# A graph layer on one core: sums stored by SyncE, a buffer for each gather, tables kept between turns, and sorted ranges of 8192 edges

## The chip, the cores and the metric

The kernel runs on one core of a Trainium2 chip. The core has five engines with instruction streams of their own: TensorE (PE; its weight loads are shown apart as PEld), VectorE (DVE), ScalarE (ACT), GpSimd (POOL) and SyncE (SP, which here issues DMAs alone). They share 16 DMA engines, an on-chip memory (SBUF, with PSUM for the products of TensorE) and the chip's HBM. The metric is the time of one execution on the device, in microseconds, as the median of several runs.

## The reference

The input is a table `x` of 100,000 nodes with 64 features, and 3,300,000 edges (`src`, `dst`), sorted by destination. The edges are 1,600,000 random pairs in both directions and one edge from each node to itself. The inputs are made from seed 0.

```
h   = relu(layernorm(x))
y_e = W @ [h[dst_e], h[src_e] - h[dst_e]] + b        for each edge e
s   = segment_sum(y, dst);  cnt = number of edges of each node
out = x + where(cnt > 0, s / max(cnt, 1), 0)
```

The product with `W` is linear, so it may be applied after the mean over a node's edges. What costs is the sum over edges of `h[src]` for each destination.

## The kernel before

Rows of `h` are kept in HBM as `h3`: three bf16 parts that add up to the float32 value, then a column of ones that counts edges. Sums go to an accumulator `acc` in HBM, 65 float32 values for each node.

The edges are divided in two. The first 256 x 7936, in the order of their destinations, make 256 *ranges* (`NW` = 256, one row of `src_w` and `dst_w` each). A range has `WL` = 8192 places; the last `PAD` = 256 hold a key `END` that sorts behind all edges. The rest of the edges, in the order of their destinations too, make 354 *chunks* of 28 x 128 edges (`NCH`, `J` = 28).

A range's sums go to `CH` = 256 rows of nodes from the range's first destination on. Chunks use 128 rows in the same way. Several tests write into a tile `odd` whether the data fit such a layout:

- lines 443 to 446: a range's last destination minus its first must be below `CH`;
- lines 628 and 629: a range may hold at most 256 edges from a node to itself;
- others hold for chunks (line 250), for counts of edges between a range and a block of sources, and for positions.

Lines 959 to 967 take the maximum over all tests as `turns`: a number of clearings, 0 or 1, and a number of passes of a general loop, 0 or `NF` = edges / 2048 rounded up.

The stages, in order of time:

1. *Opening* (lines 199 to 304): layer norm, `h3`, a float32 copy `hb`, and zeros into `acc`.
2. *Sort* (`sort_windows`): each range is sorted by source with a bitonic network on DVE and ACT, one range per half partition. Meanwhile POOL gathers rows for chunks.
3. *Pass 0* (`passes(0, ...)`, written out in full). For the 40 source blocks of group 0, tables (`tab`) of `h3` lie in SBUF. A set is four ranges, a pass does all 64 sets. Each block of a set takes `pick` (one-hot product on PE that picks the source rows), a copy by ACT to bf16, and `put` (one-hot product that adds rows into `total` in PSUM by destination). After 40 blocks `total` goes through `whole` and a reduction to `wsums`, and these partial sums go to `part_d` in HBM.
4. *Turns*: a loop of three for groups 1 to 3, then a loop of two *final halves* for group 4, with 32 sets each. A final set adds its sums to `acc`.
5. *General loop* (lines 1005 to 1055): if `turns` says so, `acc` is cleared, and then all edges are done again, 2048 in each of `NF` passes. A pass loads indices, gathers 16 x 128 rows, makes one-hot products, and adds the 16 results to `acc` with indirect accumulating DMAs issued by POOL. With data that fit, both loops run zero times.
6. *Closing stage* (lines 1057 to 1093): `acc`, `hb` and `x` are read, divided, multiplied by the weights and stored.

Chunks run beside all this as an event stream (`chunks`, line 347): one indirect gather on POOL (line 399), and, `LAGJ` = 21 gathers later, one product on PE (line 410). A pass interleaves them by a written-out rate: pass 0 by `STEP`, turns by the number of chunks `KB` = 64 that each owns. The gathers go to buffers `nb` of seven (`JN`), six such buffers in rotation. After 28 gathers the sums of a chunk (`sums`) are added to `acc` by POOL: an indirect accumulating DMA in the static part (line 368), an accumulating DMA to a loaded address in the loops (line 373). The sums of final sets go the same way (line 922). `add_later` and `add_now` hold these adds back until 14 gathers later, with at least `GAP` = 4 gathers between two of them. `in_turn`, `behind` and `issue_after` fix an instruction's place in its engine's order.

SP issues nearly all loads: `srs` and `dt` (sources and destinations of a block for the one-hots, fetched ten blocks ahead), `prev` (partial sums), `tab` at the start of each turn, the chunks' indices `si` and `di`, and the stores of `wsums` to `part_d`. At the edge of a loop all engines drain and meet.

Of the kernel before, what the change touches and what calls it, by code (L numbers as in the profile page):

```python
# [28 lines left out]
P = 128  # L29
# [3 lines left out]
KB = 64  # L33
KG = 8
JN = 7
JH = 14
LAG = 3
LAGJ = 21
GATHER = 1270
STEP = 900  # L40
GAP = 4
# [12 lines left out]
PAD = 256  # L54
# [39 lines left out]
def gnn_preln(ctx: ExitStack, tc, x, src_w, dst_w, src_p, dst_p, src_a, dst_a, wT, b, out, V, E):  # L94
# [35 lines left out]
    RT = max(R, NCB * CS)  # L130
# [6 lines left out]
    assert 2 * C == P and NX * P >= 2 * CH and PA >= 0 and KB % 2 == 0  # L137
# [6 lines left out]
    acc = dram.tile([R, C1], F32, name="acc")  # L144
# [3 lines left out]
    ksort = dram.tile([NW * WL, 1], I32, name="ksort")  # L148
# [34 lines left out]
    odd = consts.tile([P, 3 + 2 * NL + 2], F32, name="odd")  # L183
# [3 lines left out]
    hb_v = hb.rearrange("(p t) c -> p t c", p=P)  # L187
    h3_v = h3[:R].rearrange("(p t) c -> p t c", p=P)
    acc_v = acc.rearrange("(p t) c -> p t c", p=P)
# [9 lines left out]
    with tc.tile_pool(name="pre", bufs=2) as pre, tc.tile_pool(name="small", bufs=4) as small, \  # L199
# [11 lines left out]
        zeros = pre.tile([P, T, C1], F32, name="zeros", bufs=1)  # L211
        nc.gpsimd.memset(zeros, 0.0)
        for r in range(R, RT, P):
            n = min(P, RT - r)
            nc.scalar.dma_start(h3[r:r + n], zeros.rearrange("p t c -> p (t c)").bitcast(BF16)[:n, :CT])
# [90 lines left out]
    with tc.tile_pool(name="rows", bufs=6) as rows, \  # L306
# [40 lines left out]
        def chunks(first, n, dynamic=None):  # L347


            def load(q):  # L350
# [5 lines left out]
                nc.sync.dma_start(di[:, :k], dst_p[at].rearrange("k p j -> p k j"))  # L356
# [5 lines left out]
                to = index.tile([P, KG], I32, name="to", bufs=3)  # L362
                nc.vector.tensor_scalar(to[:, :k], base_b[:, at], pcol, None, op0=ALU.add)
                return si, near, to

            def addition(q, rows_to, sums):
                if dynamic is None:
                    nc.gpsimd.indirect_dma_start(
                        out=acc, out_offset=bass.IndirectOffsetOnAxis(ap=rows_to, axis=0),
                        in_=sums, in_offset=None, compute_op=ALU.add)  # L370
                else:
                    at = number(base_r[0:1, ds(dynamic + q, 1)], POOL, V)
                    nc.gpsimd.dma_start(acc[ds(at, P)], sums, accum_op=ALU.add)  # L373
# [15 lines left out]
            for e in range(n * J + LAGJ):  # L389
                q, j = divmod(e, J)  # L390
                u = q % KG
                if e < n * J:
                    if j == 0:
                        if u == 0:
                            si, near, to = ahead
                        of[q] = u, si, near, to
# [7 lines left out]
                if d + JN >= 0 and (d + JN) % JH == 0:  # L404
                    hot_of(d + JN)
# [724 lines left out]
```

## Time and profile before

| what | value |
|---|---|
| median of 3 runs | 16331.0 us (16321.65 to 16351.86) |
| the profiled execution | 16308.1 us |
| its span | 16306.4 us |
| instructions | 639004 |
| gathers of chunks (line 399) | 9912, 1025 ns mean, 10159.1 us in all |
| HBM read, written | 1655.06 MB, 255.11 MB |

The stages begin at about 0 (opening), 410 (sort), 2530 (slots are filled), 2707 (pass 0), 5261, 7782 and 10289 (turns), 12790 and 14403 (final halves) and 15993 us (closing stage).

In the groups of instructions, a row gives the line, the engine, the operation, what it writes and reads, the shapes and the count; then busy time and mean duration of one; then the idle time of the engine just before, and what ended most of it. "issue" is time in which nothing that the profile shows was waited for. A row of waits says who waited for whom, the total in us, the number of waits and the longest. A row of the timeline gives the start, the duration, the instruction, and in brackets the engine's idle time before it and what ended that. A row of a stretch gives busy time and count for PE, PEld, DVE, ACT and POOL, then the clock granted to TensorE, the DMA share and GB/s.

### The profile page before, as it was taken

The numbers are of one execution on the slowest core, as the hardware profiler recorded it, in microseconds if no ns is written. First come the engines' busy times: TensorE is split into PE (matmuls) and PEld (weight loads), VectorE is DVE, ScalarE is ACT, GpSimd is POOL, SyncE is SP. The second block draws the span as 40 slices with busy tenths as digits, with TensorE's granted clock in tenths as the row PEclk, the third lists the DMA queues.
The fourth block names the chain that finished last, engine by engine and source line by source line (L and its number), as shares of the span: only waits on it lengthen the run. The fifth ranks groups of instructions, "written<-read, shape, count | busy, mean of one in ns | idle before, by whom it ended". The sixth has DMA issues, their size and how long they took to land. (4 is left out here: it accounts for less than half of the span.)

```text
span 16306.4 us, 639004 instructions
## 1 busy us (share of the span) xinstructions
PE 12051.6 (74%) x266300; PEld 9566.6 (59%) x266300; DVE 12400.5 (76%) x31837; ACT 7270.1 (45%) x15555; POOL 11887.4 (73%) x11203
## 2 busy tenths in 40 slices
PE   6111113899996988898888899788899777767775
PEld 5001012777774777776777777677777666556654
DVE  6999997888884877787777788677788666656663
ACT  6234393555553444444444444444444333333331
POOL 4777777776656777777777777777777777767766
PEclk7555556999997999999999999899999888988887
DMA  7311124444444545554544455544455544455447
GB/s 294 82 39 39 40 59 107 121 124 124 126 123 106 126 125 125 125 127 113 144 122 125 124 127 126 130 122 125 125 128 127 128 106 106 106 117 108 106 104 260
DMA packets 1639658, 1952.46 MB, mean 120 GB/s; under 512 B 1039558, under 2 KB 1040206, under 8 KB 1631758
## 3 DMA queue, kind: packets, MB, share of 16 engines
q1 hardware_dynamic: 1178128, 1341.28, 27.4%
q0 software_dynamic: 454560, 544.34, 18.5%
q8 instruction: 2086, 34.18, 0.8%
q10 hardware_dynamic: 4032, 25.69, 0.4%
q14 instruction: 852, 6.98, 0.1%
HBM read 1655.06 MB, written 255.11 MB: 117 GB/s over the span
## 5 line engine op out<-in xcount | busy, mean ns | idle before, releaser
L399 POOL DMA_INDIRECT nb<-h,si x9912 | 10159.1, 1025 | 3436.5 <-issue 2642.3
L870 ACT CAST gs<-gp 128x386 bf16<-128x386 f32 x12800 | 5570.9, 485 | 7102.0 <-PE gp L865 6961.0
L342 DVE TENSOR_TENSOR dh<-dt,upto 128x512 bf16<-128x512 int16 x12800 | 4582.1, 420 | 1797.4 <-PE total L877 1660.3
L877 PE MATMUL total<-gs,dh 32*128 32x193 bf16 x200704 | 5465.0, 247 | 408.0 <-DVE whole L907 377.6
L865 PE MATMUL gp<-tab,gh 128*128 128x193 bf16 x50176 | 5419.6, 250 | 349.3 <-DVE gh L844 227.6
L865 PEld LDWEIGHTS <-gh 128*128 128x128 bf16 x51200 | 4487.9, 99 | 1410.2 <-issue 967.4
L877 PEld LDWEIGHTS <-dh 32*128 32x128 bf16 x200704 | 3997.4, 94 | 1479.3 <-issue 926.8
L410 PE MATMUL ps<-nb,hot 128*128 128x193 bf16 x9912 | 2231.0, 274 | 3012.8 <-DMA nb<-h,si 1519.6
L844 DVE TENSOR_SCALAR gh<-srs,who_f 128x768 bf16<-128x768 int16 (+1 forms) x10240 | 3414.6, 396 | 981.2 <-PE gp L865 846.8
L410 PEld LDWEIGHTS <-hot 128*128 128x128 bf16 x9912 | 862.6, 103 | 3281.0 <-issue 1654.0
L471 ACT COPY tmp<-keys 128x1536 f32<-128x1536 f32 (+26 forms) x525 | 647.7, 1244 | 1044.8 <-DVE keys L473 880.4
L342 DVE TENSOR_TENSOR hot<-near,upto 128x512 bf16<-128x512 int16 (+1 forms) x2832 | 915.8, 385 | 68.1 <-PE ps L410 67.5
L472 DVE TENSOR_TENSOR keys<-tmp,keys 128x1536 f32<-128x1536 f32 (+26 forms) x525 | 748.0, 1462 | 68.3 <-ACT tmp L471 67.2
L473 DVE TENSOR_TENSOR keys<-tmp,keys 128x1536 f32<-128x1536 f32 (+26 forms) x525 | 750.3, 1460 | 1.1
L910 DVE TENSOR_REDUCE wsums<-whole 128x512 f32<-128x1536 f32 x320 | 614.5, 1920 | 0.2
L765 POOL DMA_INDIRECT kw<-ksort,at x392 | 427.3, 1090 | 211.4 <-issue 94.5
L922 POOL DMA_DIRECT2D acc<-wsums x256 | 332.9, 1300 | 326.5 <-DMA acc<-wsums 305.6
L907 DVE COPY whole<-total 128x386 f32<-128x386 f32 x640 | 326.5, 552 | 49.8 <-ACT whole L905 46.4
L547 ACT ACTIVATE junk<-keys,bound 128x543 bf16<-128x543 f32 x450 | 337.3, 750 | 16.9 <-DVE keys L473 3.6
L415 DVE TENSOR_REDUCE sums<-ps 128x64 f32<-128x192 f32 x354 | 124.0, 350 | 271.0 <-PE ps L410 270.6
L905 ACT COPY whole<-total 128x386 f32<-128x386 f32 x640 | 276.4, 484 | 115.9 <-PE total L877 103.2
L373 POOL DMA_DIRECT2D acc<-sums x256 | 264.1, 1032 | 12.0 <-DVE sums L417 6.8
(170 smaller groups left out, 4258.8 us busy)
## 6 DMA issues: line engine op xcount, KB each, us to landing
srs<-sr_d SPq DMA_DIRECT2D x2560, 320.0 KB
nb<-h,si POOLq DMA_INDIRECT x9912
part_d<-wsums SPq DMA_DIRECT2D x256, 260.0 KB
prev<-part_d SPq DMA_DIRECT2D x256, 260.0 KB
tab<-h SPq DMA_DIRECT2D x92, 485.0 KB
dt<-dt_d SPq DMA_DIRECT2D x2560, 10.0 KB
h<-parts SPq DMA_DIRECT2D x28, 1358.0 KB
dt_d<-dt SPq DMA_DIRECT2D x40, 640.0 KB
```

What stands on the lines that cost most here:

```text
L342: return nc.vector.tensor_tensor(out.rearrange("p k (a d) -> p k a d", d=D), numbers[:, :, None].to_broadcast(shape), upto[:shape[0], :n]. ...
L399: last[POOL] = nc.gpsimd.indirect_dma_start(out=nbs[e // JN][:, e % JN], out_offset=None, in_=h3, in_offset=bass.IndirectOffsetOnAxis(ap=o ...
L410: in_turn(nc.tensor.matmul(ps[:, :CE], lhsT=hots_of[d // JH][:, d % JH], rhs=nbs[d // JN][:, d % JN, :CE], start=jd == 0, stop=jd == J - 1))
L471: last[ACT] = nc.scalar.copy(tmp, lo)
L472: nc.vector.tensor_tensor(lo, tmp, hi, ALU.min)
L473: last[DVE] = nc.vector.tensor_tensor(hi, tmp, hi, ALU.max)
L765: last[POOL] = nc.gpsimd.indirect_dma_start(out=kw[:, r], out_offset=None, in_=ksort, in_offset=bass.IndirectOffsetOnAxis(ap=at[:, r, s:s ...
L844: nc.vector.tensor_scalar(ghots[v, k][:, part, a:z].rearrange("p c i s -> p (c i s)"), srs[v, k][:, a:z].rearrange("p c i s -> p (c i s)") ...
L865: mm = nc.tensor.matmul(gp[:, i], lhsT=ghots[v, k][:, b, c, i], rhs=of[:, :CE], start=b == 0, stop=b == NT - 1)
L870: nc.scalar.copy(gs[t], gp)
L877: mm = nc.tensor.matmul(total[:, r, b * CE:b * CE + CE], lhsT=dh[at, i, b * P:b * P + P], rhs=rows_of[at, i, :CE], start=begin and i == 0 ...
L910: nc.vector.tensor_reduce(sums[:, :, :C], whole[:, :, :C3].rearrange("p k (s c) -> p k c s", s=3), axis=AX.X, op=ALU.add)
```

## The change

- *A buffer for each gather.* `JN` goes from 7 to 1, with `NBUF` = 35 buffers of one gather each. The one-hots of chunks are built seven gathers ahead as before (`NLEAD`).
- *Sums stored by SP.* There are two accumulators `accs`. Ranges and chunks alternate between them, so that no two neighbours write the same one; within one accumulator the rows of two ranges or chunks must not overlap, and two new tests (`apart`) go into `odd`. The sums are then stored by plain DMAs on SP in place of accumulating DMAs on POOL. Zeros go to both accumulators during the sort and not in the opening; the first 12 chunks' sums wait until then (`HELD`). `GAP` is 1. The closing stage reads both and adds them.
- *Tables kept.* `tabs` are allocated once. A pass loads the next group's table of five blocks during its last set, as soon as that table has been used; before, each turn loaded all tables at its start.
- *The end of a set.* ACT does all four copies to `whole`; the reduction is split in four and, with what follows it, is put between the one-hots of the next set (`todo`).
- *Ranges of 8192 edges.* `PAD` is 0. Ranges hold 256 x 8192 edges and 336 chunks are left, of which a turn owns 60 (`KB`). `ksort` is longer by 256 keys `END`. `CH` and the tests of before are as they were.
- *Pass 0* spreads the static chunks' remaining gathers evenly (`share`) in place of the rate by `STEP`.

```diff
-KB = 64
+KB = 60
-JN = 7
+JN = 1
+NLEAD = 7
+NBUF = 35
-LAG = 3
+HELD = 12
-STEP = 900
-GAP = 4
+GAP = 1
-PAD = 256
+PAD = 0
...
-    RT = max(R, NCB * CS)
+    RT = max(R, (NCB + NS) * CELL)
...
-    acc = dram.tile([R, C1], F32, name="acc")
+    accs = [dram.tile([R, C1], F32, name=f"acc{i}") for i in range(2)]
...
-            nc.sync.dma_start(acc_v[:, t:t + T], zeros)
...
-            def addition(q, rows_to, sums):
-                if dynamic is None:
-                    nc.gpsimd.indirect_dma_start(
-                        out=acc, out_offset=bass.IndirectOffsetOnAxis(ap=rows_to, axis=0),
-                        in_=sums, in_offset=None, compute_op=ALU.add)
-                else:
-                    at = number(base_r[0:1, ds(dynamic + q, 1)], POOL, V)
-                    nc.gpsimd.dma_start(acc[ds(at, P)], sums, accum_op=ALU.add)
+            def addition(q, sums):
+                at = number(base_r[0:1, first + q:first + q + 1] if dynamic is None else base_r[0:1, ds(dynamic + q, 1)], SP, V)
+                last[SP] = nc.sync.dma_start(accs[(first + q) % 2][ds(at, P)], sums)
...
-                        nbs[e // JN] = rows.tile([P, JN, CT], BF16, name="nb")
+                        nbs[e // JN] = rows.tile([P, JN, CT], BF16, name="nb", bufs=NBUF)
...
+            for t in range(0, NPT, T):
+                for a in accs_v:
+                    last[SP] = nc.sync.dma_start(a[:, t:t + T], zeros)
...
+            apart = piece.tile([1, NW + NCH], F32, name="apart", bufs=1)
+            nc.vector.tensor_tensor(apart[:, :NW - 2], wb_r[:, 2:], wb_r[:, :NW - 2], ALU.subtract)
...
+                if then is not None and v == n - 1 and s % SL == SL - 1:
+                    load_table(k, then)
...
-                    if r < QW // 2:
-                        nc.scalar.copy(whole[:, r], total[:, r, :NT * CE])
-                    else:
-                        nc.vector.tensor_copy(whole[:, r], total[:, r, :NT * CE])
+                    nc.scalar.copy(whole[:, r], total[:, r, :NT * CE])
...
-                for r in range(QW):
-                    def addition(w=u * QW + r, of=sums[:, r * NT:r * NT + NT]):
-                        at = number(wb_r[0:1, ds(w, 1)], POOL, V - CH)
-                        nc.gpsimd.dma_start(acc[ds(at, CH)].rearrange("(b p) c -> p b c", p=P), of, accum_op=ALU.add)
+                    for r in range(QW):
+                        def addition(w=u * QW + r, i=r % 2, of=sums[:, r * NT:r * NT + NT]):
+                            at = number(wb_r[0:1, ds(w, 1)], SP, V - CH)
+                            last[SP] = nc.sync.dma_start(accs[i][ds(at, CH)].rearrange("(b p) c -> p b c", p=P), of)
...
+                if (t + 2) % SG and t % SL < 2 and todo:
+                    with tc.issue_after(latest[0].ins):
+                        todo.pop(0)()
...
+        def load_table(k, g):
+
+            for i in range(2):
+                nc.sync.dma_start(tabs[k][:, i],
+                                  h3[ds((i * NCB + g * SG + k * SL) * CELL, SL * CELL)].rearrange("(x p) f -> p x f", p=P))
...
-                        gathers(2 * STEP - (SL // 2 * QW * 1300 + 4 * 1300) / (SG // 2))
+                        gathers(share)
...
-            at, ht, xo = loads.pop(t)
+            at, bt, ht, xo = loads.pop(t)
+            nc.vector.tensor_add(at, at, bt)
```

More of the change, by code (lines that the diff above doesn't have):

```diff
@@ L971, in gnn_preln @@
                     tc.tile_pool(name="a_ps", bufs=1, space=PSUM) as a_ps:
+                for k in range(NBT):
+                    tabs.append(load.tile([P, 2, SL * NT, CT], BF16, name=f"tab{k}", bufs=1))
+                    load_table(k, 0)
                 with tc.tile_pool(name="slots", bufs=2) as piece:
@@ L975, in gnn_preln @@
                         next(fill)
-                    for i, _ in enumerate(passes(0, SETS, 0, False)):
+                    share = (PA * J - count[0]) * GATHER / (SETS * SG // 2)
+                    for i, _ in enumerate(passes(0, SETS, 0, False, 1)):
                         if i % (SG // 2) == 0:
@@ L985, in gnn_preln, with turn @@
                 add_now(True)
[L987 removed]
+                def turn(g, n, base, at, kb, final, then=None):
                     last.pop(PE, None)
[L989 removed]
+                    ev = chunks(PA, kb, at)
                     next(ev)
                     owed = 0.0
[L992 removed]
+                    for _ in passes(g, n, base, final, then):
                         owed += 2 * (kb * J - 1) / (n * SG)
```

105 lines of the change are left out of this document (55 added, 50 removed).

## The prediction

> **What bounds the kernel now.** I read the busy totals, then the stretches between the engines' long pauses, then what POOL and PE waited for inside them.
>
> ```profile
> PE 12051.6 (74%) x266300; PEld 9566.6 (59%) x266300; DVE 12400.5 (76%) x31837; ACT 7270.1 (45%) x15555; POOL 11887.4 (73%) x11203
> 410.00:2530.00 2120.00, 315.02 (x1555) 204.03 (x1552) 1996.06 (x2457) 1020.38 (x1426) 1598.87 (x1619) 0.50 0.22 51
> 5049.00:5261.00 212.00, 70.40 (x835) 36.81 (x823) 39.99 (x128) 14.12 (x33) 150.98 (x154) 0.58 0.40 87
> 5261.00:7782.00 2521.00, 2221.02 (x52992) 1772.84 (x52992) 1953.50 (x5593) 1160.87 (x2688) 1953.46 (x1880) 0.97 0.50 126
> 12790.00:14403.00 1613.00, 1195.14 (x25217) 953.46 (x25216) 996.12 (x2830) 587.01 (x1344) 1145.49 (x1089) 0.88 0.51 109
> 15993.00:16306.40 313.40, 202.28 (x1176) 183.08 (x1176) 133.13 (x220) 56.16 (x112) 200.40 (x56) 0.80 0.84 322
> ```
>
> The stretches (columns: PE, PEld, DVE, ACT, POOL busy, clock, DMA share, GB/s) are the sort, the end of pass 0, one turn, one half of the final turn, and the closing stage. No engine is full over the span. The sort belongs to DVE (1996 of 2120 us). In a turn POOL looks 77% busy, and yet it is the bound:
>
> ```profile
> L399 POOL DMA_INDIRECT nb<-h,si x1787 | 1860.4, 1041 | 544.4 <-issue 473.7 <-PE gp L865 32.6 <-DMA nb<-h,si 26.5
> L373 POOL DMA_DIRECT2D acc<-sums x64 | 66.4, 1038 | 2.3 <-DVE sums L417 2.2
> PE ps L410 <- DMA nb<-h,si: 162.4, 199, 2.5
> L399 POOL DMA_INDIRECT nb<-h,si x869 | 890.3, 1025 | 271.5 <-issue 241.4 <-DMA nb<-h,si 11.6 <-PE gp L865 7.9
> L922 POOL DMA_DIRECT2D acc<-wsums x128 | 166.2, 1298 | 161.9 <-DMA acc<-wsums 152.5 <-issue 7.1 <-DVE sums L417 2.2
> L830 POOL DMA_INDIRECT rows_x<-h,xs x32 | 31.2, 974 | 14.7 <-issue 9.4 <-DMA xs<-xs_d 5.2
> PE ps L410 <- DMA nb<-h,si: 310.7, 194, 10.3
> ```
>
> The first three rows are turn 1, the rest the first final half. In turn 1 POOL's work and idle time add up to the whole stretch, and its idle time is the steady 0.3 us between gathers: a gather costs (1860.4 + 544.4) / 1787 = 1.346 us, and PE waits 162 us for gathers. In the final half the stores of sums stand in the same queue, each held until the one before has landed (152.5 us).
>
> **The part of the change that decides.** `PAD` goes from 256 to 0, so each of the 256 sorted ranges holds 8192 edges where it held 7936. A range's sums go into `CH` = 256 rows of nodes. Lines 443 to 446 compare each range's last destination minus its first with `CH`; one range at 256 or more sets `odd`, line 967 then makes the count `NF`, and the general loop at line 1021 does all edges over again after the accumulators are cleared. The change leaves that test and `CH` alone. An average node has 3,300,000 / 100,000 = 33 edges, so a range of 7936 spans about 240 nodes and one of 8192 about 248. The inputs are fixed by seed 0, so this can be counted: sort the destinations, cut the first 256 x 8192 into rows, take last minus first. Mean 248.1, spread 3.0, and four rows (numbers 70, 152, 226 and 237, from 0) give 256, 257, 256 and 256. With 7936 the largest is 250. A second test (line 629, edges from a node to itself over 256 in one range) also trips: 259 in the worst range, 252 with 7936. Now neither does, and the trace shows the loops skipped, the closing loads following the last sum within 11 us:
>
> ```profile
> 15975.02 0.86 POOL L373 DMA_DIRECT2D acc<-sums  x1 [2.47 <-DMA acc<-wsums]
> 15978.95 1.57 DVE L1010 MEMSET zeros<- 128x1820 f32 x1 [18.54 <-SPq L1011]
> 15985.82 0.34 SPq L1064 DMA_DIRECT2D at<-acc  x1
> ```
>
> So I expect the changed kernel to run its fast part and then the general loop, NF = 3,300,000 / 2048 rounded up = 1612 times. The sum is therefore the fast part, a clearing, and 1612 passes of a loop that this trace never enters.
>
> **The fast part.** Chunks outside the ranges fall from 354 to 336 (28 gathers each), in a turn from 64 to 60.
>
> Turns: POOL needs 1680 x 1.346 = 2261 us, and the 64 adds leave it for SP. PE without its gather waits needs 2472 - 162 = 2310 us, so PE is late next. Keeping the tables takes most of the pause between turns (51 us, below) off; with 12 us for the restart a turn takes about 2320, against 2521: about 195 less, three times, 585.
>
> ```profile
> 7782.43 0.34 PE L865 MATMUL gp<-tab,gh 128*128 128x193 bf16 x1 [51.31 <-DVE gh L844]
> PE total L877 <- DVE whole L907: 76.8, 59, 2.7
> L905 ACT COPY whole<-total 128x386 f32<-128x386 f32 x640 | 276.4, 484 | 115.9 <-PE total L877 103.2
> L910 DVE TENSOR_REDUCE wsums<-whole 128x512 f32<-128x1536 f32 x320 | 614.5, 1920 | 0.2
> ```
>
> Final halves: POOL 840 x 1.337 + 32 x 1.43 = 1169 us without the stores, PE 1553 - 311 = 1242 at most; about 1240 in place of 1600, 720 for both. Pass 0: gathers are spread evenly, so most of the 212 us of draining at 5049 goes, some 165. Its indirect adds leave POOL too. The set's end: all four `whole` copies go to ACT, 4 x 0.484 = 1.9 us where ACT and DVE shared them, at worst 0.9 us more on each of 64 sets a turn, 58 us; the 1.92 us reduction is split so that DVE can build one-hots between its parts, worth up to that row's 76.8 us of PE waits. I take the two as even. A buffer for each gather (35 for 42) changes when PE may start, and POOL has 35 x 1.35 = 47 us of lead as its cover; nothing.
>
> Stores moved to SP: each waits there for the earlier one to the same accumulator, and the loads of `srs`, `dt` and `prev` stand behind it. Two accumulators alternate and loads run ten blocks ahead (about 10 x 0.96 = 9.6 us), so a wait like POOL's 152.5 / 63 = 2.4 us is covered; if the four stores of a final set came in one block, 4 x 2.4 = 9.6 us, that cover would be used up. Bounds 0 and 64 x 9.6 = 614 us; I take 0.
>
> Opening and sort: 28 stores of zeros (910 KB) leave the opening, whose DMA runs at 293 GB/s, and 56 enter the sort (DMA share 0.22) on SP, ahead of some index loads: 51 MB at 293 GB/s is 174 us. Bounds -87 and +174; even, 0. Closing stage: 28 more loads of 910 KB at its 322 GB/s are 79 us, 28 more additions of 2.02 us on DVE hide beneath; +79.
>
> ```profile
> 0.00:410.00 410.00, 270.57 (x1567) 228.85 (x1568) 264.53 (x199) 246.69 (x337) 201.48 (x96) 0.78 0.78 293
> acc<-zeros SPq DMA_DIRECT2D x28, 910.0 KB
> L1075 DVE TENSOR_TENSOR mean<-at,cnt 128x1792 f32<-128x1792 f32 x27 | 54.5, 2020 | 0.9
> ```
>
> Fast part: 16306 - 585 - 720 - 165 + 79 = 14,915 us. Lower bound 14,570, with POOL's 2273 a turn and 1181 a half and the opening's 87; upper bound 15,700, with SP's 614 and the sort's 174.
>
> **The general loop.** One pass, on POOL: 16 gathers, then 16 indirect adds into one accumulator (lines 1030 to 1055), then a loop edge at which every engine drains. Nearest rows, the end of the first final half with its loop edge, and the indirect adds of the static chunks:
>
> ```profile
> 14348.44 1.18 POOL L922 DMA_DIRECT2D acc<-wsums  x1 [2.16 <-DMA acc<-wsums]
> 14351.75 1.19 POOL L922 DMA_DIRECT2D acc<-wsums  x1 [2.13 <-DMA acc<-wsums]
> 14355.11 1.21 POOL L922 DMA_DIRECT2D acc<-wsums  x1 [2.17 <-DMA acc<-wsums]
> 14358.72 0.88 POOL L373 DMA_DIRECT2D acc<-sums  x1 [2.41 <-DMA acc<-wsums]
> 14368.66 1.07 POOL L399 DMA_INDIRECT nb<-h,si  x1 [9.06 <-DMA si<-in_src_p]
> 14372.67 0.94 POOL L399 DMA_INDIRECT nb<-h,si  x1 [0.30 <-issue]
> 10253.10 1.06 POOL L399 DMA_INDIRECT nb<-h,si  x1 [12.38 <-DMA si<-in_src_p]
> L368 POOL DMA_INDIRECT acc<-sums,to x98: 1577/1627/3857, 547.5 to 5251.6; - x98
> ```
>
> - Edge and index load: 9.06 us from the last add's issue to the first gather; the larger loop's is 12.38. I take 9.1, the shorter body.
> - Gathers: 16 x 0.95 + 15 x 0.30 = 19.7, and 0.3 before the adds.
> - Adds: 16 x 1.63 (median of the last row) = 26.1.
> - Between adds: all go to one accumulator, so each waits for the landing of the one before, 2.13 to 2.17 us after its issue in those rows, which carry two rows of nodes a partition. The loop's carry one; I take 1.9. Ends: 0.3 (no wait) and 2.5. 15 x 1.9 = 28.5.
> - DVE's comparisons (three operations on 128 x 2048, some 2.3 us each by the 2.02 us row) and PE's 16 products lie under the gathers.
>
> One pass: 9.1 + 19.7 + 0.3 + 26.1 + 28.5 = 83.7 us; 1612 passes are 134,900. Clearing: 56 stores, 51 MB at 293 GB/s, 174 us. Sum: 14,915 + 174 + 134,900 = 149,990 us. That is made against an execution of 16,308 us (span 16,306), 0.1% below the median 16,331 of the runs shown; here this is nothing.
>
> The Trainium skill, in "DMA: Bandwidth & Descriptors" (Rules for kernel authors), says an accumulating DMA must wait for the semaphore of an earlier one on the same bytes, as the same queue does not order them. The trace agrees with 152.5 us of such waits. The same page (Anatomy of one DMA) prices a DMA at 2.0 us plus bytes / 436 GB/s; for 33 KB that is 2.08, an estimate by which the pass would be 86.4 us and the sum about 154,400.
>
> **Rivals.**
> 1. The test does not trip, and only the fast part counts: 14,915 us, faster by 8.5%. The mechanism is POOL relieved of 18 chunks and of every add; it decides if no range spans 256 nodes or more. For it speaks that the mean, 248, is below 256; against it four counted ranges, and a spread of 3.0, by which the limit is only 2.5 spreads off while 256 ranges are drawn.
> 2. The loop's adds do not wait for each other: 9.1 + 19.7 + 16 x (1.63 + 0.3) = 59.7 us a pass, 111,300 in all. For it: the L368 adds show no such wait, though they stood 28 gathers apart; against it the L922 rows.
> 3. Everything in the loop at its upper end (12.4 for the edge, 1.71 an add, 2.5 between): 12.4 + 20 + 27.4 + 37.5 = 97.3 us, 172,700 with a fast part of 15,700.
> 4. The spreading stores on SP hold up its loads: the fast part ends at 15,700 or so, within the forecast's range; by itself (with rival 1) still faster than now.
>
> **How the numbers follow.** Forecast 0.70, rival 1 0.06, rival 2 0.12, rival 3 0.12; rival 4 lies within them. The time is the forecast's, 150,000. The range 108,000 to 173,000 takes in rivals 2 and 3, with 3 ms below rival 2 for a cheaper edge; the forecast's own range is 140,000 to 160,000. A measurement here can tell some 0.2%. Slower holds 0.94, faster 0.06, the same nothing.
>
> **What would show it.** Right: the general loop's gathers and adds appear, 16 x 1612 = 25,792 of each, with a loop period near 84 us, adds some 3.5 us apart, POOL idle half of the span. The fast part: turns near 2320 us, final halves near 1240, no draining after pass 0, no adds on POOL before the general loop. Wrong: the closing loads follow the last store at once; then the count of spans above or my reading of the test is at fault. A period of 60 us would say that the adds overlap, one of 100 that the edge or the landing is dearer here.

## The result, and the profile after

The changed kernel takes 162,758.9 us in the median of four runs (162,742.04 to 162,762.64), beside 16,341.43 us for the kernel before (16,321.65 to 16,356.92): 9.96 times as long, with a 95% interval of 9.943 to 9.978. Forecast were 150,000 us, with 140,000 to 160,000 for the forecast's own case and 108,000 to 173,000 over all cases. The profiled execution took 162,742.04 us, with a span of 162,740.2.

The page of the changed kernel: its span, the busy totals, POOL in 40 slices, and the costliest groups of the general loop:

```profile
span 162740.2 us, 979509 instructions
PE 19785.4 (12%) x291588; PEld 12065.6 (7%) x291588; DVE 34489.4 (21%) x69041; ACT 11599.0 (7%) x41987; POOL 82081.5 (50%) x61672
POOL 6776444444444444444444444444444444444444
L1077 POOL DMA_INDIRECT acc<-sums,ti x25792 | 40237.5, 1560 | 58551.6 <-ACT sums L1076 46447.7
L1055 POOL DMA_INDIRECT nb<-h,si x25792 | 31030.3, 1203 | 18174.3 <-DMA si<-in_src_a 10658.9
L1059 DVE TENSOR_TENSOR same<-dr,di 128x2048 bf16<-128x2048 int32 x1612 | 5741.9, 3562 | 0.0
L1062 DVE TENSOR_TENSOR prior<-same,before 128x2048 f32<-128x2048 bf16 x1612 | 3694.7, 2292 | 55.6
L1064 DVE TENSOR_REDUCE first<-prior 128x16 f32<-128x2048 f32 x1612 | 3669.6, 2276 | 0.0
```

The new rows are the message. L1055, L1059 and L1077 are lines of the general loop, which did not exist in the profile before; their counts, 1612 and 25,792 = 16 x 1612, say that it ran from end to end. It fills slices 5 to 40 of POOL's row, at four or five tenths busy.

Stretches of the changed kernel that answer to those of before (columns: PE, PEld, DVE, ACT, POOL busy, clock, DMA share, GB/s): turn 1, the first final half, the clearing, and the closing stage.

```profile
5062.00:7358.00 2296.00, 2168.33 (x52880) 1745.76 (x52880) 1897.18 (x5608) 1207.47 (x2816) 1772.86 (x1680) 0.99 0.56 135
11966.00:13173.00 1207.00, 1095.25 (x25160) 885.78 (x25159) 956.43 (x2835) 604.12 (x1408) 927.73 (x872) 0.98 0.64 137
14356.00:14499.00 143.00, 0.00 (x0) 0.00 (x0) 2.83 (x7) 0.00 (x0) 0.00 (x0) 0.50 0.91 374
162349.00:162740.20 391.20, 214.10 (x1176) 195.15 (x1176) 193.49 (x252) 56.92 (x112) 200.65 (x56) 0.74 0.84 331
```

The fast part did become faster, by about what was forecast: 14,356 us before the clearing and 391 behind the loop, 14,747 together, where 14,915 were forecast and the kernel before took 16,306. The stage times that can be set against the forecast:

| stage | before | forecast | after |
|---|---|---|---|
| end of pass 0 | 5261 | 165 earlier | 5062, 199 earlier |
| a turn | 2521, 2507, 2501 | 2320 | 2296, 2310, 2298 |
| both final halves | 1613 + 1590 | 720 less | 1207 + 1183, 813 less |
| closing stage | 313 | 392 | 391 |
| clearing | none | 174 | 143 |
| one pass of the general loop | none | 83.7 | 91.72 |

All else, 162,347 - 14,499 = 147,848 us, is the general loop. One pass of it on the timeline of POOL and DVE (start, duration, instruction, and in brackets the idle time before it with what ended that); the first four rows are the last adds of the pass before, and rows of the same kinds are left out between the shown ones:

```profile
80056.20 1.55 POOL L1077 DMA_INDIRECT acc<-sums,ti  x1 [2.32 <-ACT sums L1076]
80060.07 1.56 POOL L1077 DMA_INDIRECT acc<-sums,ti  x1 [2.32 <-DMA acc<-sums,ti]
80064.04 1.55 POOL L1077 DMA_INDIRECT acc<-sums,ti  x1 [2.40 <-DMA acc<-sums,ti]
80067.91 1.56 POOL L1077 DMA_INDIRECT acc<-sums,ti  x1 [2.32 <-DMA acc<-sums,ti]
...
80076.02 1.02 POOL L1055 DMA_INDIRECT nb<-h,si  x1 [6.55 <-DMA si<-in_src_a]
80077.35 0.98 POOL L1055 DMA_INDIRECT nb<-h,si  x1 [0.31 <-issue]
80078.62 3.56 DVE L1059 TENSOR_TENSOR same<-dr,di 128x2048 bf16<-128x2048 int32 x1
80078.63 0.94 POOL L1055 DMA_INDIRECT nb<-h,si  x1 [0.30 <-issue]
80079.88 3.07 POOL L1055 DMA_INDIRECT nb<-h,si  x1 [0.30 <-issue]
80082.21 2.29 DVE L1062 TENSOR_TENSOR prior<-same,before 128x2048 f32<-128x2048 bf16 x1
80083.26 2.06 POOL L1055 DMA_INDIRECT nb<-h,si  x1 [0.30 <-issue]
80084.69 2.28 DVE L1064 TENSOR_REDUCE first<-prior 128x16 f32<-128x2048 f32 x1
80085.63 0.94 POOL L1055 DMA_INDIRECT nb<-h,si  x1 [0.30 <-issue]
...
80099.36 1.62 POOL L1077 DMA_INDIRECT acc<-sums,ti  x1 [0.30 <-issue]
80103.43 1.58 POOL L1077 DMA_INDIRECT acc<-sums,ti  x1 [2.45 <-ACT sums L1076]
```

The shape is the forecast's: an edge, 16 gathers, 16 adds that stand about 4 us apart. Two things in it are not. The gather at 80079.88 takes 3.07 us and the one at 80083.26 2.06, where the others take 0.94 to 1.02; both began while a DVE operation of line 1059 or 1062 was running. (The gather at 80078.63 began 0.01 us after the operation of line 1059 and took 0.94 all the same.) And the idle time between the adds is 2.3 to 2.45 us, not 1.9.

From the groups above, per pass: adds 16 x 1.560 = 24.96; idle before adds 58551.6 / 1612 = 36.32, of which 0.30 stands before the first, so 36.0 / 15 = 2.40 between two of them; gathers 16 x 1.203 = 19.25; idle before gathers (18174.3 - 145.4 at the loop's entry) / 1612 = 11.18, of which 10658.9 / 1611 = 6.62 is the edge. Together 91.7 us.

| term of a pass | forecast | measured | times 1612 |
|---|---|---|---|
| edge and index load | 9.1 | 6.62 | -4.0 ms |
| gathers and their gaps | 19.7 | 23.82 | +6.6 ms |
| adds | 26.1 | 24.96 | -1.8 ms |
| between adds (and 0.3 before) | 28.5 + 0.3 | 36.32 | +12.1 ms |
| pass | 83.7 | 91.72 | +12.9 ms |

The loop's 12.9 ms less the 0.2 ms by which fast part and clearing were cheaper are the whole miss of 12.75 ms (162,742 - 149,990).

### The profile page after: what moved, and what is told of

It reads as the page before. It is cut to its first block, busy times and chain, and to the rows that moved or that the text cites. A ratio compares the mean times of both kernels' runs of the same rounds, so it can differ in the third digit from the quotient of the medians.

```text
span 162740.2 us, 979509 instructions
## 1 busy us (share of the span) xinstructions
PE 19785.4 (12%) x291588; PEld 12065.6 (7%) x291588; DVE 34489.4 (21%) x69041; ACT 11599.0 (7%) x41987; POOL 82081.5 (50%) x61672
## 5 line engine op out<-in xcount | busy, mean ns | idle before, releaser
L1077 POOL DMA_INDIRECT acc<-sums,ti x25792 | 40237.5, 1560 | 58551.6 <-ACT sums L1076 46447.7
L1055 POOL DMA_INDIRECT nb<-h,si x25792 | 31030.3, 1203 | 18174.3 <-DMA si<-in_src_a 10658.9
L1075 DVE TENSOR_REDUCE sums<-ps 128x64 f32<-128x192 f32 x25792 | 9163.6, 356 | 88662.6 <-DMA acc<-sums,ti 88662.2
L1073 PE MATMUL ps<-nb,same 128*128 128x193 bf16 x25792 | 8094.4, 332 | 139868.4 <-DVE same L1059 67553.2
L1076 ACT COPY sums<-ps 128x1 f32<-128x1 f32 x25792 | 4108.7, 159 | 143893.7 <-DVE sums L1075 143893.7
L1073 PEld LDWEIGHTS <-same 128*128 128x128 bf16 x25792 | 2666.6, 109 | 145293.3 <-DVE same L1059 74245.4
L395 POOL DMA_INDIRECT nb<-h,si x9408 | 9830.9, 1045 | 3323.9 <-issue 983.5
L1059 DVE TENSOR_TENSOR same<-dr,di 128x2048 bf16<-128x2048 int32 x1612 | 5741.9, 3562 | 0.0
L1062 DVE TENSOR_TENSOR prior<-same,before 128x2048 f32<-128x2048 bf16 x1612 | 3694.7, 2292 | 55.6
L1064 DVE TENSOR_REDUCE first<-prior 128x16 f32<-128x2048 f32 x1612 | 3669.6, 2276 | 0.0
L345 DVE TENSOR_TENSOR hot<-near,upto 128x384 bf16<-128x384 int16 (+1 forms) x2688 | 879.7, 384 | 21.0 <-PE ps L406 18.1
```

The source lines that it names most:

```text
L345: return nc.vector.tensor_tensor(out.rearrange("p k (a d) -> p k a d", d=D), numbers[:, :, None].to_broadcast(shape), upto[:shape[0], :n]. ...
L395: last[POOL] = nc.gpsimd.indirect_dma_start(out=nbs[e // JN][:, e % JN], out_offset=None, in_=h3, in_offset=bass.IndirectOffsetOnAxis(ap=o ...
L1055: nc.gpsimd.indirect_dma_start(out=nb[:, j], out_offset=None, in_=h3, in_offset=bass.IndirectOffsetOnAxis(ap=si[:, j:j + 1], axis=0))
L1059: nc.vector.tensor_tensor(same, dr.rearrange("q p j -> q j p"), di[:, :, None].to_broadcast([P, JA, P]), ALU.is_equal)
L1062: nc.vector.tensor_mul(prior, same, before[:, None, :].to_broadcast([P, JA, P]))
L1073: nc.tensor.matmul(ps, lhsT=same[:, j], rhs=nb[:, j, :CE], start=True, stop=True)
```

## The experiments

The theory after the result: the ranges of 8192 edges alone set off the general loop (1); in it the adds wait for the landing of the one before, because all go to one accumulator (2); its gathers are held while DVE compares (3); and the other parts of the change are worth what the stages show (4). Rivals stood against each: another part of the change sets off the loop or makes it dearer; the adds wait for ACT, as the rows name it; the long gathers come from HBM or from the indices.

One thing has to be known first. The experiments ran on four chips. On three of them the kernel before took 24,300 us and not 16,340, and the changed kernel without its general loop 18,560, steadily; runs of one kernel on one chip agree within 0.4%, and the runs in which the general loop was changed or put into the kernel before are one execution each. So each ratio is one of kernels on the same chip, and times from different chips are not set against each other, except for the pass of the general loop, which took the same on the two chips where it ran unchanged (below). Expectations in us that were made for the other pace can be held only against differences. The last heading comes back to this.

### Ranges of 8160 edges: the change without the loop

```diff
-PAD = 0
+PAD = 32
```

With 32 keys of padding, the widest range counted from the inputs spans 255 nodes, under the limit of 256, and the most edges from a node to itself in one range are 256, which is just allowed. Everything else of the change stays.

> The changed kernel with PAD = 32 in place of 0 and nothing else: ranges of 8160 edges, 338 chunks in place of 336. Counted from the inputs of seed 0, the widest range spans 255 (the limit is 256) and the most edges from a node to itself in one range are 256 (the limit is to be over 256). Theory (the tests on a range's width send the changed kernel into the general loop): the loop does not run, and the time is the changed kernel's without it, 162,743 - 1612 x 91.72 - 145 of clearing = 14,750 us, some 50 more for two chunks at most; 14,700 to 14,850. Rival (another test trips, such as the two new ones on neighbours in one accumulator, which 32 keys change by nothing): the loop runs, about 162,800 us.

Measured: 18,560.32 us (18,531.7 to 18,563.56), 0.7629 of the kernel before on that chip (0.7616 to 0.7642; 24,321.94). No instruction of lines 1055 to 1077 is in the trace. A padding of 32 keys in place of none takes the loop away, so the length of the ranges had set it off. That it did so through the tests on a range's width and on its edges from a node to itself rests on the counts from the inputs; both tests change sides between the two paddings, and they were not tried apart. The time in us was missed, for the chip's pace; the ratio shows a faster kernel all the same.

Two repeats beside other kernels, on the two other chips of that pace, gave 18,566.88 us (0.7641, 0.7628 to 0.7653) and 18,563.55 us (0.7621, 0.7608 to 0.7633).

> The same kernel as e1_pad32. On the chip of that run the kernel before took 24,322 us where it had taken 16,341, the one-core program's long written-out stages alone being slower (in the rows of PE, stretches with a product each 0.7 us and nothing waited for), while the general loop of its neighbours ran at its old pace. Theory (that belongs to that chip and not to the kernels): beside a kernel before of 16,340 it takes 14,750, 14,700 to 14,850. Rival (the changed kernel's fast part is itself unsteady): again 18,500.

> The kernel with PAD = 32 once more, to stand beside f1_seven (14,839), f2_split (14,877) and f3_pool_stores (15,198), which ran where the kernel before takes 16,314. Theory, as for e1_pad32: 14,750, 14,700 to 14,850. If the buffers of seven and the split copies cost what they seem to, it is 14,700 to 14,800; if they are even with it, 14,830 to 14,880.

### The kernel before, with ranges of 8192 edges alone

```diff
-KB = 64
+KB = 60
-PAD = 256
+PAD = 0
...
+    ksort, longer by 256 keys END, as in the change
```

> The kernel before with PAD = 0, KB = 60 (336 chunks) and 256 keys END behind ksort; one accumulator, adds by POOL, buffers of seven, tables loaded each turn as before, and none of the new tests. Theory: the longer ranges alone cause it. The general loop runs 1612 times at about 91.7 us; the fast part loses 4 chunks a turn, 112 x 1.346 = 151 us each and 75 for a half, 16,306 - 3 x 151 - 2 x 75 = 15,700; with one clearing of 26 MB, some 75: about 163,600 us. Rival (the new tests or the stores by SP are the cause): no loop, about 15,700 us.

Measured: 172,061.52 us, the same 1612 passes. The groups of the general loop in this run, whose lines are 1035 and 1057 there:

```profile
L1057 POOL DMA_INDIRECT acc<-sums,ti x25792 | 40237.9, 1560 | 58670.7 <-ACT sums L1056 46540.1 <-DMA acc<-sums,ti 11634.5 <-issue 496.1
L1035 POOL DMA_INDIRECT nb<-h,si x25792 | 30915.8, 1199 | 18113.2 <-DMA si<-in_src_a 10743.7 <-issue 7170.5 <-DMA nb<-h,si 199.0
```

They agree with the changed kernel's within 0.4% in busy and in idle time; a pass takes 91.73 us here and 91.72 there. So the sorted ranges alone turn the kernel before into the slow one, and no other part of the change adds to the loop. The expected 163,600 was missed by 8.5 ms, because on this chip the part before the loop took 23,870 us and not 15,700; the loop itself, 147.9 ms, came as expected.

### Two accumulators in the general loop

```diff
-                    out=accs[0], out_offset=bass.IndirectOffsetOnAxis(ap=ti[:, j:j + 1], axis=0),
+                    out=accs[j % 2], out_offset=bass.IndirectOffsetOnAxis(ap=ti[:, j:j + 1], axis=0),
```

> The changed kernel with the general loop's sixteen adds going to the two accumulators in turn; the closing stage adds both as before. Theory (each add waits until the one before it to the same accumulator has landed, 2.40 us after its issue of 1.56): two adds a period of 3.96, so 16 adds take about 32 us in place of 61 and a pass 62 to 63; total 162,743 - 1612 x 29 = 116,000 us, 112,000 to 121,000. Rival 1 (adds wait for the sums that ACT writes, which the rows of the waits name): a pass stays at 91.7, 162,700 us. Rival 2 (the landing itself takes longer when two are under way, as when POOL's queue is the limit): a pass between 70 and 90, 130,000 to 160,000.

Measured: 118,647.27 us, with 62.06 us a pass, as expected. The idle time before the adds falls from 58,551.6 us to 10,775.8, in the groups of this run:

```profile
L1077 POOL DMA_INDIRECT acc<-sums,ti x25792 | 40244.9, 1560 | 10775.8 <-ACT sums L1076 8384.0 <-issue 2371.3 <-DMA acc<-sums,ti 20.6
```

The work that ACT and DVE do for a sum is the same in both kernels, only the destination changed. So the 46.4 ms that the changed kernel's row puts down to ACT's copy of `sums` were no wait for ACT's speed: each add waited for the landing of the one before on the same accumulator. The row names ACT because a copy happened to end last by the records. The changed kernel's own timeline above says the same: its last three adds of a pass, for which no copy is left to be made, wait 2.32 to 2.40 us like the others, and there the row names the DMA of the add before. This is also what rival 2 of the prediction would have looked like (59.7 us a pass): a pass of 62.06 us is what the loop takes when neighbouring adds are free of each other, and in the changed kernel they are not.

### The product `prior` three times

```diff
-            nc.vector.tensor_mul(prior, same, before[:, None, :].to_broadcast([P, JA, P]))
+            for _ in range(3):
+                nc.vector.tensor_mul(prior, same, before[:, None, :].to_broadcast([P, JA, P]))
```

> The changed kernel with DVE's product prior done three times in each pass of the general loop. In the changed kernel two of the 16 gathers take 3.07 and 2.06 us in place of 0.94, and each ends 0.8 us after an operation of DVE with two inputs in SBUF (same, prior) that was running. Theory (a gather is held while such an operation runs): each further prior of 2.29 us holds one further gather, which then ends a period of 2.3 later in place of 1.25: two more gathers at about 2 us, a pass longer by 2.1 us, 162,743 + 3,400 = 166,100 us; the products are otherwise under cover, since the first add comes 15 us after prior. Rival (the two long gathers belong to the start of a pass, with the 1 MB load of dr or the restart of the queue): two long gathers as before, 162,700 us.

Measured: 170,363.0 us, with 94.14 us a pass, 2.42 more than without the two products (expected 2.1). The group of its gathers, and then its timeline of POOL and DVE:

```profile
L1055 POOL DMA_INDIRECT nb<-h,si x25792 | 34960.9, 1355 | 18178.7 <-DMA si<-in_src_a 10647.3 <-issue 7332.1 <-DMA nb<-h,si 199.3
```

```profile
80070.22 3.56 DVE L1059 TENSOR_TENSOR same<-dr,di 128x2048 bf16<-128x2048 int32 x1
80070.26 4.30 POOL L1055 DMA_INDIRECT nb<-h,si  x1 [0.31 <-issue]
80073.82 2.29 DVE L1063 TENSOR_TENSOR prior<-same,before 128x2048 f32<-128x2048 bf16 x1
80074.86 2.06 POOL L1055 DMA_INDIRECT nb<-h,si  x1 [0.30 <-issue]
80076.29 2.28 DVE L1063 TENSOR_TENSOR prior<-same,before 128x2048 f32<-128x2048 bf16 x1
80077.23 2.16 POOL L1055 DMA_INDIRECT nb<-h,si  x1 [0.30 <-issue]
80078.76 2.28 DVE L1063 TENSOR_TENSOR prior<-same,before 128x2048 f32<-128x2048 bf16 x1
80079.70 2.16 POOL L1055 DMA_INDIRECT nb<-h,si  x1 [0.30 <-issue]
80081.23 2.28 DVE L1065 TENSOR_REDUCE first<-prior 128x16 f32<-128x2048 f32 x1
80082.16 0.94 POOL L1055 DMA_INDIRECT nb<-h,si  x1 [0.30 <-issue]
```

Read the gathers against DVE: the one issued at 80070.26 ends at 80074.56, 0.78 us after `same` (80073.78); the next three end at 80076.92, 80079.39 and 80081.86, each 0.81 or 0.82 us after a `prior`. The gather at 80082.16 lies inside the reduction and takes 0.94 us. The long gathers follow the products: two products more make two gathers more of 2.16 us. HBM and the indices are unchanged, so the rival falls. The groups give the same: (34,960.9 - 31,030.3) / 1612 = 2.44 us a pass.

Another rival is that any long operation of DVE, or any that writes as much, holds a gather. The sort in the changed kernel's trace speaks against it. Its products (lines 475 and 476) write 128 x 1488 float32 values, but one of their two inputs, `tmp`, lies in PSUM:

```profile
1003.86 1.71 DVE L475 TENSOR_TENSOR keys<-tmp,keys 128x1488 f32<-128x1488 f32 x1
1004.01 0.94 POOL L395 DMA_INDIRECT nb<-h,si  x1 [0.30 <-DMA nb<-h,si]
```

The gather begins and ends inside the product and takes 0.94 us. The gathers between 600 and 2200 us, beside such products, take 0.950 us in the mean. In turn 1, beside one-hots of some 0.4 us with both inputs in SBUF, it is 1.055; that these hold the gathers too was not tried.

The Trainium skill, in "SBUF — State Buffer" (Who interferes with whom), says that a DVE instruction with two SBUF inputs contends with a GpSimd instruction that reads SBUF, and that a reduction never contends on this chip. The trace agrees with both, with 2.06 to 4.30 us beside 0.94, for an indirect DMA whose indices lie in SBUF. The same section also tells of a probe in which a product of two tensors did not stall a DMA; for these indirect gathers the measurement says otherwise. That the indices are what is read there was not tried.

### Ranges of 7936 edges in the changed kernel

```diff
-KB = 60
+KB = 64
-PAD = 0
+PAD = 256
```

> The changed kernel with PAD = 256 and KB = 64, both as before: 354 chunks, 98 of them static; the rest of the change stays. No range is too wide, so no general loop. Theory (in turns POOL is the bound as soon as its gathers cost more than PE's work, which is 2300 us a turn by the changed kernel's trace): a turn is 1792 x 1.346 + 12 = 2425 us in place of 2301, a half 896 x 1.337 + 46 + 12 = 1256 in place of 1195; 14,750 + 3 x 124 + 2 x 61 = 15,240 us. Rival (PE's work sets the turn's length either way, and 112 gathers more add only their products, 0.09 us each): 14,750 + 50 = 14,800.

Measured, beside the repeat with 8160 edges on that chip: 19,076.85 us (19,058.49 to 19,095.2) against 18,566.88, 510 more. That is the price of 16 more chunks, 448 gathers at 1.14 us. A turn with its four more chunks (112 gathers) takes 3146 to 3163 us against 3007 to 3012. The size is near the theory's 490, but the theory's reason doesn't hold on this chip. In the first turn of the kernel with 7936 edges POOL waits for PE and not PE for gathers, and PE has pauses that nothing in the profile explains:

```profile
POOL nb L395 <- PE gp L867: 596.0, 752, 3.9
PE total L879 <- issue: 375.5, 842, 5.7
```

So at that chip's pace the larger ranges were worth some 500 us of the fast part, for a reason that stays open; at the pace of the runs of the result this was not measured.

### One part undone at a time, without the loop

These three are the kernel with 8160 edges and one part put back, on a chip where the kernel before takes 16,313.83 us, which is the pace of the result.

Buffers of seven gathers:

```diff
-JN = 1
+JN = 7
-NBUF = 35
+NBUF = 5
```

> The kernel with PAD = 32, with buffers of seven gathers (JN = 7, five of them, 35 gathers as with a buffer each). The prediction put a buffer for each gather at nothing. Theory: the same time as e1_again, 18,567, within 60. Rival (a gather must wait until all seven products of its buffer are done, so POOL runs up to six gathers less ahead, and a set's end costs PE more): 100 to 400 us more.

Copies to `whole` shared by ACT and DVE, as before:

```diff
+                    if r < QW // 2:
+                        nc.scalar.copy(whole[:, r], total[:, r, :NT * CE])
+                    else:
+                        nc.vector.tensor_copy(whole[:, r], total[:, r, :NT * CE])
-                    nc.scalar.copy(whole[:, r], total[:, r, :NT * CE])
```

> The kernel with PAD = 32, with two of a set's four copies to whole back on DVE; the split reduction stays. The prediction took ACT's longer copying (at worst 0.9 us a set) and the split reduction as even. Theory (PE waits for the last copy, and two engines copy sooner): faster by up to 0.9 us on each of 256 sets, 18,340 to 18,567. Rival (DVE's copies keep its one-hots back): slower by 0.55 x 2 us a set, up to 280 us more.

Sums stored by POOL, still plain stores to two accumulators (both places):

```diff
-                last[SP] = nc.sync.dma_start(accs[(first + q) % 2][ds(at, P)], sums)
+                last[POOL] = nc.gpsimd.dma_start(accs[(first + q) % 2][ds(at, P)], sums)
...
-                            last[SP] = nc.sync.dma_start(accs[i][ds(at, CH)].rearrange("(b p) c -> p b c", p=P), of)
+                            last[POOL] = nc.gpsimd.dma_start(accs[i][ds(at, CH)].rearrange("(b p) c -> p b c", p=P), of)
```

> The kernel with PAD = 32, with the plain stores of sums issued by POOL in place of SP. Theory (they stand in the gathers' queue there, about 1.04 us each for a chunk's and 1.30 for a range's, with the wait for an earlier store's landing on top): 60 a turn, 62 us where POOL has some 40 us to spare, and 30 + 128 in a half, 31 + 166 us and up to 150 of waits: 3 x 30 + 2 x (180 to 330) = 450 to 750 us more than 18,567. Rival (SP's stores delay its loads as much as they would POOL's gathers): the same time or faster.

| kernel | us | to before | turns | both halves |
|---|---|---|---|---|
| buffers of seven | 14,838.91 | 0.9096 (0.9066 to 0.9126) | 2303, 2303, 2298 | 2431 |
| shared copies | 14,876.96 | 0.9119 (0.9079 to 0.9160) | 2329, 2334, 2330 | 2383 |
| stores by POOL | 15,198.46 | 0.9316 (0.9273 to 0.9360) | 2340, 2341, 2335 | 2641 |
| the changed kernel (the run of the result) | - | - | 2296, 2310, 2298 | 2390 |

The waits of PE in one turn (us in all, times, longest), first in the changed kernel, then with shared copies, and then in the first final half of the changed kernel:

```profile
PE ps L406 <- DMA nb<-h,si: 57.0, 66, 2.3
PE total L879 <- ACT whole L908: 46.8, 57, 1.0
```

```profile
PE total L879 <- DVE whole L911: 107.4, 63, 6.3
PE ps L406 <- DMA nb<-h,si: 23.7, 28, 2.4
```

```profile
PE ps L406 <- DMA nb<-h,si: 64.2, 80, 3.0
```

And the first final half with stores by POOL: POOL's stores among the groups, and PE's waits for gathers:

```profile
L926 POOL DMA_DIRECT2D acc<-wsums x127 | 96.2, 758 | 30.1 <-DMA acc<-wsums 20.7 <-issue 7.9 <-DMA acc<-sums 1.0
```

```profile
PE ps L406 <- DMA nb<-h,si: 150.8, 128, 3.5
```

POOL's gathers in turn 1, first in the changed kernel, then with shared copies:

```profile
L395 POOL DMA_INDIRECT nb<-h,si x1680 | 1773.2, 1055 | 523.3 <-PE gp L867 185.0 <-issue 128.0 <-PE ps L406 95.1
```

```profile
L395 POOL DMA_INDIRECT nb<-h,si x1680 | 1805.1, 1074 | 524.0 <-PE gp L867 185.3 <-issue 136.2 <-PE ps L406 81.1
```

In both, POOL's busy and idle time add up to the whole turn (2296.5 of 2296 us and 2329.1 of 2329), and the idle time is 0.31 us for each gather. So POOL's gathers still fill a turn of the changed kernel.

- *Buffers*: no more than some 50 us in the halves or in pass 0, nothing in the turns.
- *Copies by ACT*: giving two copies back to DVE costs some 30 us a turn and nothing in the halves (2383 beside 2390), the direction of the rival. PE's waits for `whole` grow by 60.6 us, its waits for gathers shrink by 33.3. POOL, which fills the turn, spends 31.9 us more on the same 1680 gathers (1.074 us each in place of 1.055); why they last longer was not tried. The split reduction was not undone, so its share is not known.
- *Stores by SP*: on POOL they cost 37 us a turn and 251 in the halves, where PE's waits for gathers rise from 64 us to 150.8 in the first. It is some 360 us in all against the kernel with buffers of seven (which differs in its buffers too), where 450 to 750 were expected.

The fastest of all kernels run is the one with buffers of seven and 8160 edges: 14,839 us, 9% under the kernel before and 11 times as fast as the changed one. The kernel with 8160 edges and single buffers met only the slower chips; at this pace an estimate is 14,800: the 14,747 of the changed kernel without its loop, and some 50 for its two more chunks and a later start of pass 0.

### Tables loaded at the start of each turn

```diff
-                if then is not None and v == n - 1 and s % SL == SL - 1:
-                    load_table(k, then)
...
+            if not starts:
+                for k in range(NBT):
+                    load_table(k, g)
```

> The kernel with PAD = 32, with all tables loaded at the start of each turn and half, as before, and not during the last set of the one before. Theory: PE's pause at a turn's edge grows back from the changed kernel's 36 to 42 us towards the 51 to 99 us of before, in three turns and two halves: 5 x (15 to 45) = 75 to 225 us more than e1_third. Rival (the pause is the edge's own and the first one-hots', and the tables land beside it): within 30 us.

Measured, beside the third run with 8160 edges on that chip: 18,594.01 us (18,583.56 to 18,604.45) against 18,563.55, 30 more, at the edge of what the rival allowed and not the 75 to 225 expected. The pauses did come back as the theory had it. PE's pause at the second edge, first with the tables loaded there, then in the run beside it:

```profile
9031.55 0.34 PE L867 MATMUL gp<-tab,gh 128*128 128x193 bf16 x1 [46.97 <-issue]
```

```profile
8970.12 0.34 PE L867 MATMUL gp<-tab,gh 128*128 128x193 bf16 x1 [14.94 <-DMA dt<-dt_d]
```

At the five edges the pauses are 47.0 to 56.7 us in place of 14.0 to 15.8, some 177 more together. Most of that was made up within the turns, by what is not shown. This was on a chip of the slower pace, so what the loads cost at the other one is not settled.

### The kernel before once more

> The kernel before, unchanged, where it takes 24,300 us: its profile, to see where the 8,000 us stand that the first trace of it (16,306) lacks. Theory 1 (the engines' sequencers pause there, so that stages with most instructions a us grow most): turns and halves grow by the same factor as PE's step, every engine shows pauses that nothing released, and a gather keeps its 1.04 us. Theory 2 (POOL's gathers themselves are slower): a gather takes 1.5 us or more.

Measured: 16,329.78 us, on the chip of the three runs above. It was meant to show what makes it 24,300 us elsewhere; it met a chip where it isn't, and so tells nothing of that.

## Why the prediction was right or wrong

- **The part that decides**: right. Counting the spans of the ranges from the inputs told that the test trips; 1612 passes ran. A padding of 32 keys ended it in the changed kernel, and ranges of 8192 edges brought it into the kernel before. Rival 1 fell with that.
- **The general loop, between adds** ("I take 1.9"): the step that failed most. The mechanism, a wait for the landing of the add before, is shown by the run with two accumulators. The size was 2.40 us, +12.1 ms. The prediction took three rows with 2.13 to 2.17, for direct adds with two rows of nodes a partition, and went below them because the loop's adds carry one. That had no row behind it. Yet the same prediction works out the mean of all such waits in that half, 152.5 / 63 = 2.4 us, for the stores on SP. With that mean the term would have been right: 15 x 2.4 = 36 us. The upper end of 2.5 held it. The formula of the Trainium skill in "DMA: Bandwidth & Descriptors" (Anatomy of one DMA), quoted in the prediction, gave 2.08 for this: nearer than 1.9, and still short of the measured 2.40.
- **"DVE's comparisons ... lie under the gathers"**: wrong as a step. In time they do, but they hold the gathers: +4.1 us a pass, +6.6 ms, shown by the run with three products. `same` also takes 3.56 us where the 2.02 us row had been taken for some 2.3.
- **Edge** (9.1): 6.62. The row taken, 9.06, belonged to a loop with a larger body. **Adds** (1.63): 1.56; the median of the 98 adds of before was a little high. These two gave 5.8 ms back.
- **The fast part** (14,915): 14,747, the sum right within 1.2%, in part by luck. "PE is late next" (2310 us of PE against 2261 of POOL) was wrong. POOL still fills the turn: its gathers cost 2296.5 / 1680 = 1.367 us in place of 1.346, and PE without its 57.0 us of waits for gathers would need only 2239. The POOL row of the experiments shows the former, PE's waits the latter. Two errors met near 2320. The final halves gained 813 us for 720. Of "I take the two as even" at the set's end, the run with shared copies shows a gain of some 30 us a turn from the copies.
- **Stores on SP** (0, bounds 0 and 614): 0 is consistent with halves that came out below the forecast; no load waited long enough to show. **A buffer for each gather** (nothing): no effect in the turns, at most some 50 us elsewhere. **Tables**: PE's longest wait at the edge fell from 51.31 us to 12.12, as forecast:

```profile
7358.60 0.34 PE L867 MATMUL gp<-tab,gh 128*128 128x193 bf16 x1 [12.12 <-DMA dt<-dt_d]
```

- **Opening and sort** (0): pass 0 begins at 2709 us in place of 2707. **Clearing** (174 by 293 GB/s): 143, at 374 GB/s. **Closing** (+79): 391 for 392.

So the forecast's case came, 12.75 ms over its value and 2.7 ms over its own range, within the range over all cases. The two missed terms pull the same way, 18.7 ms together. That the two that were too dear hid a third of it is luck. The wider range held because it took in rival 3, with every term at its upper end.

## What to carry to other kernels

A constant that sizes a tile may also be the input of a test that chooses between a fast and a slow path: look for what the data do to that test, with the data, before costing any instruction. When consecutive accumulating DMAs go to one tensor, alternate between two; here that took a pass from 91.7 to 62.1 us. An operation that lies beside a DMA-issuing engine in time may still hold it: look at the duration of each issue, by its position in the loop, and not only at the mean. For a wait that a group of rows has many of, take the mean of the group before a few picked rows.

## What the runs showed of the hardware that was not expected

- Indirect gathers issued by POOL last until about 0.8 us after one of the loop's DVE products with two SBUF inputs that was running when they began: 2.06 to 4.30 us in place of 0.94. One that began 0.01 us after the product was not held, one that began 0.04 us after it was. A reduction of 2.28 us doesn't hold them, and neither do the sort's products of 1.71 us with one input in PSUM.
- An accumulating indirect DMA of 128 rows of one node each has the next one on the same tensor wait 2.40 us after its issue. The direct ones with twice the rows had 2.42 in the mean of 63 waits in the kernel before, so no row shows that less to carry lands sooner (the kinds of DMA differ, and a load alone was not varied).
- On some chips the long static part runs at another pace. The kernel before took 24,300 us on three of the four chips of the experiments and 16,314 on the fourth; the changed kernel with 8160 edges took 18,560 on those three, and 14,839 with buffers of seven on the fourth. The general loop did not change (91.73 and 91.72 us a pass). The clock granted to TensorE was 0.95 in a turn of 3007 us there and 0.99 in the 2296 us here, too near to explain it. In the third run with 8160 edges the group of PE's largest products looks like this:

```profile
L879 PE MATMUL total<-gs,dh 32*128 32x193 bf16 x200704 | 6601.4, 252 | 2123.5 <-issue 1511.3 <-ACT whole L908 578.1 <-DVE dh L345 12.1
```

  PE stands idle for 1511 us before these products with nothing that the profile shows to wait for. No run here tested what holds it up, and why it differs from chip to chip stays open.
